# Cross-attention: the second batch's queries of chunks 6 to 9 by seven products for eight, with new softmax sets and a new hand-written order

## The chip, the cores and the metric

The kernel runs on one core of a Trainium2 chip. The metric is device time in microseconds of one execution. Three runs of the kernel before took 495.48, 495.83 and 495.85 us, with a median of 495.83. The engines are called as the profile calls them: PE is TensorE, DVE VectorE, ACT ScalarE, POOL GpSimd, SP the queue that issues DMAs.

## The reference

Two batches of 2048 tokens with 640 channels attend to 154 context rows of 1024 channels. The first 77 context rows are text, the other 77 image rows; each has its own softmax, and the two results are added. There are 20 heads of 32 channels. Everything is fp32.

```python
q    = split_heads(x @ Wq.T)
k, v = split_heads(text @ Wk.T), split_heads(text @ Wv.T)
k_ip, v_ip = split_heads(ip @ Wk_ip.T), split_heads(ip @ Wv_ip.T)
out  = merge(attend(q, k, v)) + merge(attend(q, k_ip, v_ip))
y    = out @ Wo.T + bo + x
```

## The kernel before

**Tiling.** The 640 channels are five chunks of 128, four heads each. Chunk number q counts both batches: 0 to 4 are the first batch's, 5 to 9 the second's. A chunk's 2048 tokens are four blocks of 512; a unit u is half a chunk, 1024 tokens in two blocks (u, h), so chunk q holds units 2q and 2q+1. A unit's scores come in three groups s of 3, 3 and 2 token tiles (of 128), 12 or 8 rows of heads and tiles, each with 2 x 77 scores.

**Stages of a chunk.** `queries` (line 206) makes a block's queries: five matmuls of 512 columns, one for each chunk of input channels, summed in one PSUM bank. `take_queries` (220) scales them into SBUF on ACT. `scores` (242) works on 32-row tiles of the array, four heads at once, into four banks. Then comes the softmax: for most groups ACT copies the scores (254), DVE takes maxima (290), POOL subtracts them (304), ACT takes exponentials (310), DVE sums (315) and inverts (320), POOL multiplies (325) and DVE transposes (332). Three sets of (unit, group) choose otherwise. In `DIRECT` the maxima are taken and the exponentials read straight from PSUM. In `BIASED` the copy stays, but the maximum is the bias of small exponentials (278, one row of 77 each). Both leave out POOL's subtraction. In `SUMMED` these small exponentials also accumulate the sums, which takes the sum from DVE. `attend` (341) multiplies a whole chunk with the values, again on 32-row tiles, 160 records in the profile; it is written A.q below.

**Output.** The first batch's output projection already uses seven products for eight (lines 480 to 530), with sums of attention halves on POOL (440) and of weights (410). The second batch's, after attend 9, is a longer scheme of sums (866, 872), 512-column products (887) and additions to the residual (827, 830).

**Buffers.** x has four buffers of 512 tokens, `xs[0]` to `xs[3]`. For the second batch the fourth, `xs[XROOM]`, holds sums of weights, and blocks of x are loaded anew for each chunk into the other three in turn (line 188). Three weight buffers `wqs` take Wq's chunks in turn (194). A value tile `vT` with its transposed copies `vS0` belongs to the first batch. The residual of the second batch is what the last loads left in the three x buffers, and one more load.

**What sets the order.** Nothing is scheduled by a tool: a string `SCHEDULE` names each step, and `emit` writes it to its engine; each engine runs its own steps in that order. `q.u.h@n` makes queries in bank n, `cq` takes them; `R` is scores, `K M S E D I N T` the softmax steps in the order above, `A` and `CA` attend and its copy; `LX`, `LQ`, `VS`, `SF`, `SS` issue DMAs on SP (x, Wq, values, residual in, output); `m`, `cm`, `G`, `W` are the first batch's output products, their additions and sums; `V`, `X`, `F`, `Y` the second's.

Of the kernel before, what the change touches and what calls it, by code (L numbers as in the profile page):

```python
# [20 lines left out]
def kernel(  # L21
# [31 lines left out]
    NH = 2  # L53
    BLK = NH * TB
# [10 lines left out]
        (11, 0), (12, 0), (13, 0), (13, 2), (14, 0), (14, 2), (15, 1), (15, 2), (18, 1), (19, 2),  # L65
    }
    BIASED = {
        (2, 2), (3, 2), (4, 2), (6, 2), (8, 2), (9, 2), (11, 2), (12, 1), (16, 2), (17, 2), (18, 2),
    }
    SUMMED = {  # L70
        (4, 2), (11, 2), (12, 0), (13, 0), (13, 2), (14, 0), (15, 1), (15, 2), (16, 2), (17, 2), (18, 1),
        (18, 2), (19, 2),
# [13 lines left out]
    halves = banks[:G], banks[G:]  # L86
# [16 lines left out]
    vT = const.tile([P, B, LP], F32, name="vT")  # L103
    nc.gpsimd.memset(vT[:, :, 2 * L :], 0.0)
    vS0 = [const.tile([P, LP], F32, name=f"vS0_{n}") for n in range(2)]
# [108 lines left out]

    def take_queries(u, h, pq):
        if (u, h) in EARLY:
            qT = aT[:, EARLY[u, h]]
        else:
            qT = qpool.tile([P, TB], F32, tag="qT", name=f"qT_{u}_{h}")
        nc.scalar.mul(qT, pq, SCALE)  # L220
        qTs[(u, h)] = qT
# [48 lines left out]
    def exponential_of(u, s, ps=None, den=None):  # L270

        n = GROUPS[s][1]
        for g in range(G):
            for t in range(n):
                for x in range(2):
                    row = rows_of(u, s)[:, t * G + g, x]
                    one = t * G + g, slice(x, x + 1)
                    nc.scalar.activation(  # L278
                        row,
                        row if ps is None else rows_in(ps[g], n)[:, t, x],  # L280
                        AF.Exp,
                        bias=maxs[(u, s)][:, *one],
                        accum_out=None if den is None else den[:, *one],
                    )
# [148 lines left out]
    def sum_t(m, b, i):  # L433
# [6 lines left out]
        nc.gpsimd.tensor_tensor(t_of(m, b, i), x, y, ALU.subtract)  # L440
# [144 lines left out]
    for t in range(2):  # L585

        ps = halves[t][G - 2 + t]
# [76 lines left out]
    def emit(word):  # L664
        name, _, where = word.partition("@")
        k, *args = name.split(".")
        x, y = (*(int(a) for a in args if a.isdigit()), None, None)[:2]
        i = int(k[1:]) if k[1:].isdigit() else None
        if k[0] == "R":
            at[name] = halves[int(where)]  # L670
            scores(x, i, at[name])
        elif k == "A":
# [263 lines left out]
```

## Time and profile before

| | |
|---|---|
| median of three runs | 495.83 us |
| span of the profiled execution | 494.6 us |
| HBM read, written | 54.94 MB, 10.49 MB |
| mean granted TensorE clock | 1.000 |

The profile is one execution, so its span and not the median is what its rows add up to; the runs' median lies 1.2 us above it. In rows that group instructions, the columns are line, engine, operation, output<-input, shape and count, then busy time in us, mean ns of one, and the idle time just before them with what ended it. In rows by stage there follow, after the stretch and its length, the busy times of PE, weight loads, DVE, ACT and POOL with their counts, the granted clock, the DMA share and GB/s. An fp32 matmul leaves two records.

### The profile page before, as it was taken

To read this page: it belongs to the slowest core of one execution; us is meant where nothing else is said; L and a number is where in the kernel's file an instruction comes from. 1 tells how busy PE (TensorE), PEld (TensorE's weight loads), DVE (VectorE), ACT (ScalarE), POOL (GpSimd) and SP (SyncE) were. 2 spreads that over 40 slices of the span, in tenths; PEclk is the share of its full clock that TensorE was granted. 3 is DMA by queue.
4 is the path that set the end of the run, shared out by engine and by line. 5 is a ranking of instruction groups with operands and counts; after the bars stand their busy time and mean duration, and the time that the engine had idled before them with its cause. 6 is when DMAs were issued, how large, how long until landed. Compare 5 with 4: busy or idle time off the path is not lost.

```text
span 494.6 us, 10484 instructions
## 1 busy us (share of the span) xinstructions
PE 489.1 (99%) x4116; PEld 287.7 (58%) x4116; DVE 413.9 (84%) x416; ACT 309.5 (63%) x1002; POOL 370.5 (75%) x158
## 2 busy tenths in 40 slices
PE   9999999999999999999999999999999999999997
PEld 5666648558557556456566654754755675444443
DVE  0069989989899989979988896687789898999996
ACT  1275788977687778677899786587889862100000
POOL 0069988988988988879886758475689899798700
PEclk9999999999999999999999999999999999999999
DMA  8992046203241724895540666455550212320125
GB/s 278 350 288 80 17 124 181 67 1 95 62 150 44 247 65 146 270 345 178 161 172 27 215 195 223 134 172 183 184 169 19 90 42 85 129 85 2 42 85 212
DMA packets 67105, 69.38 MB, mean 140 GB/s; under 512 B 5488, under 2 KB 47088, under 8 KB 67056
## 3 DMA queue, kind: packets, MB, share of 16 engines
q1 hardware_dynamic: 66048, 67.54, 43.7%
q10 hardware_dynamic: 1008, 1.18, 0.7%
q8 instruction: 32, 0.52, 0.4%
q14 instruction: 17, 0.14, 0.1%
HBM read 54.94 MB, written 10.49 MB: 132 GB/s over the span
## 4 chain that ended last, share of the span: by engine, by line
PE 96%; DMA 3%; ACTq 0%; ACT 0%; DVE 0%; DVEq 0%; issue 0%
PE bank L206 34%; PE bank L887 12%; PE bank L341 11%; PE bank L242 11%; PE bank L499 10%; PE bank L144 9%; PE bank L480 7%; PE bank L509 3%; DMA aT<-in_L_xattn_Wk_ip_dram 2%; DMA x<-in_x_dram 1%; ACTq L538 0%; ACT pb L254 0%; ACTq L552 0%; DVE acc L830 0%; DVEq L931 0%
## 5 line engine op out<-in xcount | busy, mean ns | idle before, releaser
L325 POOL TENSOR_TENSOR pb<-pb,rden 128x1848 f32<-128x1848 f32 (+1 forms) x60 | 176.0, 2943 | 30.4 <-DVE rden L320 23.6
L304 POOL TENSOR_TENSOR pb<-pb,mx 128x1848 f32<-128x1848 f32 (+1 forms) x39 | 121.6, 3129 | 55.4 <-DVE mx L290 55.3
L206 PE MATMUL bank<-x,wq 128*128 128x512 f32 x280 | 125.4, 598 | 0.1
L332 DVE STREAM_TRANSPOSE pb<-pb 128x1920 f32<-128x1920 f32 (+1 forms) x60 | 115.9, 1938 | 9.1 <-POOL pb L325 8.9
L290 DVE TENSOR_REDUCE mx<-pb 128x24 f32<-128x1848 f32 (+1 forms) x50 | 91.6, 1844 | 32.1 <-ACT pb L254 31.9
L254 ACT COPY pb<-bank 128x462 f32<-128x462 f32 (+1 forms) x200 | 85.3, 542 | 29.3 <-PE bank L242 28.9
L315 DVE TENSOR_REDUCE den<-pb 128x24 f32<-128x1848 f32 (+1 forms) x47 | 88.9, 1895 | 15.6 <-ACT pb L310 12.8
L206 PEld LDWEIGHTS bank<-x,wq 128*128 128x128 f32 x280 | 51.7, 190 | 60.0 <-issue 58.8
L310 ACT ACTIVATE pb<-pb 128x1848 f32<-128x1848 f32 (+1 forms) x39 | 65.6, 1684 | 17.5 <-POOL pb L304 17.4
L278 ACT ACTIVATE pb<-bank,mx 128x77 f32<-128x77 f32 x208 | 60.4, 387 | 6.5 <-DVE mx L293 6.5
L278 ACT ACTIVATE pb<-pb,mx 128x77 f32<-128x77 f32 x184 | 54.1, 356 | 1.9 <-DVE mx L290 1.8
L341 PE MATMUL bank<-pb,v 32*32 32x512 f32 x1600 | 55.2, 597 | 0.0
L206 PE MATMUL bank<-x,aT 128*128 128x512 f32 x116 | 51.8, 596 | 0.0
L242 PEld LDWEIGHTS bank<-kT,qT 32*128 32x128 f32 x1024 | 36.1, 184 | 21.6 <-issue 13.3
L144 PE MATMUL bank<-wo_ct,aT 128*128 128x154 f32 x320 | 46.0, 297 | 0.7 <-DMA aT<-in_L_xattn_Wk_ip_dram 0.4
L144 PEld LDWEIGHTS bank<-wo_ct,aT 128*128 128x128 f32 x320 | 43.0, 188 | 4.7 <-issue 3.0
L242 PE MATMUL bank<-kT,qT 32*128 32x154 f32 x1024 | 45.1, 305 | 0.0
L278 ACT ACTIVATION_READ_ACCUMULATOR pb<-bank,mx 128x1 f32 x168 | 44.0, 266 | 0.0
L341 PEld LDWEIGHTS bank<-pb,v 32*32 32x32 f32 x1600 | 29.0, 103 | 22.7 <-issue 10.1
L480 PE MATMUL bank<-aT,wo_ct 128*128 128x512 f32 x80 | 36.3, 595 | 0.0
L206 PEld LDWEIGHTS bank<-x,aT 128*128 128x128 f32 x116 | 21.4, 190 | 23.7 <-issue 23.5
L220 ACT ACTIVATE qT<-bank 128x512 f32<-128x512 f32 x32 | 19.3, 631 | 23.4 <-PE bank L206 23.4
(83 smaller groups left out, 524.2 us busy)
## 6 DMA issues: line engine op xcount, KB each, us to landing
x<-in_x_dram SPq DMA_DIRECT2D x20, 1280.0 KB, 6.7
out_dram<-acc SPq DMA_DIRECT2D x19, 256.0 KB, 2.9
x<-in_x_dram SPq DMA_DIRECT2D x17, 256.0 KB, 5.9
acc<-in_x_dram SPq DMA_DIRECT2D x16, 256.0 KB, 4.4
out_dram<-x SPq DMA_DIRECT2D x15, 256.0 KB, 2.0
v<-vS SPq DMA_DIRECT2D x160, 20.0 KB, 2.7
aT<-in_L_xattn_Wk_dram SPq DMA_DIRECT2D x5, 512.0 KB, 6.0
aT<-in_L_xattn_Wk_ip_dram SPq DMA_DIRECT2D x5, 512.0 KB, 5.5
```

Source lines behind the costliest of these rows:

```text
L144: nc.tensor.matmul(keys_in(out), loaded[n][:, k, :], cT[:, k, :, t, :], start=(k == 0), stop=(k == NCC - 1))
L206: nc.tensor.matmul(pq, weight_of(q)[:, k, :], xs[place_of(u, h)][:, k, :], start=(k == 0), stop=(k == NC - 1), skip_group_check=loose,)
L242: nc.tensor.matmul(ps[g][:, ts(t, 2 * L)], qTs[(u, h)][g * D : (g + 1) * D, ts(st, P)], kT[g * D : (g + 1) * D, c, b].rearrange("p t l -> ...
L254: nc.scalar.copy(keys_of(u, s)[:, :, g], ps[g][:, : n * 2 * L].rearrange("p (n l) -> p n l", n=n))
L278: nc.scalar.activation(row, row if ps is None else rows_in(ps[g], n)[:, t, x], AF.Exp, bias=maxs[(u, s)][:, *one], accum_out=None if den i ...
L290: nc.vector.tensor_reduce(mx, rows_of(u, s), AX.X, ALU.max, negate=negate)
L304: nc.gpsimd.tensor_tensor(rows_of(u, s), rows_of(u, s), maxs[(u, s)].unsqueeze(3).to_broadcast([P, n, 2, L]), ALU.subtract)
L315: nc.vector.tensor_reduce(den_of(u, s), rows_of(u, s), AX.X, ALU.add)
L325: nc.gpsimd.tensor_tensor(rows_of(u, s), rows_of(u, s), rdens[(u, s)].unsqueeze(3).to_broadcast([P, n, 2, L]), ALU.mult)
L332: nc.vector.transpose(p, p)
L341: nc.tensor.matmul(pa[r][g * D : (g + 1) * D, :], v4s[q % 2][rows, g, k, :], zones[rows, :, g, k, :], start=(k == 0), stop=(k == NK - 1),)
L480: nc.tensor.matmul(ps, wo[:, k, ts(NC - 1, P)], rows_of_attention(b, k)[:, i], start=(k == 0), stop=(k == NC - 1),)
```

## The change

**Queries in pairs.** Chunk 5 keeps its queries as they are. Chunks 6 and 7, and 8 and 9, are made in pairs, block by block of 512 tokens: four of the five chunks of input channels, as a 2 x 2 scheme (output chunk by half of the input, token half by half of the input), take seven products in place of eight; the fifth chunk of input channels is added by four more matmuls. POOL makes the sums of token halves, partly in place in x, and the sums of weights, in place in `wqs`; ACT writes the first part of each quarter of the queries and DVE adds the others. In the order string these steps are `U` (sums of weights), `h` (sums of tokens), `g` (products) and `cg` (their results).

```diff
+    spare = xs[XROOM - 1]
+    t1_spare = v_sb[:, : 2 * HT].rearrange("p (kp t) -> p kp t", kp=2)
+    s4_room = xs[XROOM].rearrange("p k t -> p (k t)")[:, ds(18 * P, 2 * P)]
+    def pair_weights(p):
+        q = NC + 1 + 2 * p
+        a, c, third = (wqs[(q + n) % 3] for n in range(3))
+        return {
+            1: a[:, 0:2],
+            2: a[:, 2:4],
+            3: s4_room.rearrange("p (kp o) -> p kp o", kp=2),
+            4: c[:, 2:4],
+            5: third[:, 0:2],
+            6: third[:, 2:4],
+            7: c[:, 0:2],
+            8: (a[:, NC - 1], c[:, NC - 1], third[:, NC - 1]),
+        }
+    def sum_pair_weights(n, p, eng):
+        w = pair_weights(p)
+        out, x, y, f = (
+            (w[5], w[7], w[4], ALU.add),
+            (w[6], w[5], w[1], ALU.subtract),
+            (w[7], w[1], w[7], ALU.subtract),
+            (w[3], w[2], w[6], ALU.subtract),
+            (w[8][2], w[8][0], w[8][1], ALU.subtract),
+        )[n]
+        eng.tensor_tensor(out, x, y, f)
+    def unit_of(p, i):
+        return SUB * (NC + 1 + 2 * p) + i // NH, i % NH
+    def pair_tokens(p, i):
+        x = xs[place_of(*unit_of(p, i))]
+        b11, b12, b21, b22 = (x[:, 2 * k : 2 * k + 2, SIDES[t]] for k in range(2) for t in range(2))
+        return {1: b11, 2: b21, 3: b22, 4: b21, 5: t1_spare, 6: b11, 7: b12}, (b11, b12, b21, b22), x
+    def sum_pair_tokens(m, p, i, eng):
+        t, (b11, b12, b21, b22), _ = pair_tokens(p, i)
+        x, y = {5: (b12, b11), 6: (b22, t[5]), 7: (b22, b12), 4: (b21, t[6])}[m]
+        eng.tensor_tensor(t[m], x, y, ALU.subtract)
+    def pair_product(m, p, i, ps):
+        w, (t, _, x) = pair_weights(p), pair_tokens(p, i)
+        part = ps[:, :HT]
+        for kp in range(2):
+            nc.tensor.matmul(
+                part,
+                w[m][:, kp],
+                t[m][:, kp],
+                start=(kp == 0 and m in (1, 2, 5)),
+                stop=(kp == 1 and m in (1, 6, 7)),
+                skip_group_check=True,
+            )
+        if m in (2, 3, 4, 5):
+            n, side = {2: (0, 0), 5: (1, 1), 3: (2, 1), 4: (1, 0)}[m]
+            nc.tensor.matmul(
+                part, w[8][n], x[:, NC - 1, SIDES[side]], start=False, stop=True, skip_group_check=True
+            )
+    def take_pair_product(m, p, i, ps):
+        second, side = {1: (0, 0), 2: (0, 0), 6: (0, 1), 3: (0, 1), 5: (1, 1), 7: (1, 1), 4: (1, 0)}[m]
+        u, h = unit_of(p, i)
+        t = query_of(u + SUB * second, h)[:, SIDES[side]]
+        if m in (1, 6, 5, 4):
+            nc.scalar.mul(t, ps[:, :HT], SCALE)
+        else:
+            nc.vector.scalar_tensor_tensor(t, ps[:, :HT], SCALE, t, ALU.mult, ALU.add)
```

**Buffers.** The later chunk's queries wait in x's third buffer; so x is loaded into two buffers in turn from the second batch's fifth block on, each block of a pair once for both chunks, and the residual of three blocks is loaded anew before the last stage (`LH`). The temporary sum of tokens lies where the first batch's values were.

```diff
+    HOMES = (1, 3, 2)
-        return late.index((u, h)) % XROOM if b else sub * NH + h
+        n = late.index((u, h))
+        return (0, 1, 2, 0)[n] if n < NHB else (n + 1) % 2
+            elif b and c and c % 2 == 0:
+                qTs[(u, h)] = spare[:, (sub * NH + h + NHB * (c == NC - 1)) % NC]
-    home = {}
+    home = {i: xs[n] for n, i in enumerate(HOMES)}
+    def load_home(n):
+        tokens = ds(S + HOMES[n] * TB, TB)
+        nc.sync.dma_start(out=xs[n], in_=xT[:, tokens].rearrange("(k p) t -> p k t", p=P))
```

**Sets and order.** `DIRECT` shrinks from 10 to 7 groups, `BIASED` grows from 11 to 16 and `SUMMED` from 13 to 16. Small exponentials are issued by quarters of a group (`E.s.u.g`), scores and attend take any four banks in place of one half of PSUM, and the whole `SCHEDULE` is new.

```diff
-            at[name] = halves[int(where)]
+            at[name] = [banks[int(n)] for n in where]
-        "co.0 T0.10 R2.11@0 K1.11 m5.0@4 I1.10 K2.11 D0.11 N1.10 R1.12@0 M2.11 q.13.0@7 K1.12 I0.11 T1.10 VS.6.1 "
+        "cq.11.0 R2.10@0472 T0.9 K2.10 U0.0 R1.10@1365 h5.0.0 g1.0.0@0 K1.10 T1.9 U1.0 g2.0.0@2 h6.0.0 cg1.0.0 "
```

What this does to the engines is shown at three places. First PE, where the kernel before makes queries of chunks 6 and 7 (wq is the chunk's weights, x_82 to x_85 are x's four buffers):

```order
L206 MATMUL bank_72<-x_83,wq_76 128x512 x5
L206 MATMUL bank_74<-x_84,wq_75 128x512 x5
L499 MATMUL bank_71<-aT,x_85 128x256 x2
L509 MATMUL bank_71<-aT,x_85 128x256
L499 MATMUL bank_71<-aT,x_85 128x256 x2
L509 MATMUL bank_71<-aT,x_85 128x256
```

And PE now, at the first products of the first pair, just before attend 4 (v_sb is the temporary sum of tokens):

```order
L281 MATMUL bank_67<-x_83,wq_75 128x256 x2
L281 MATMUL bank_69<-x_83,wq_75 128x256 x2
L291 MATMUL bank_69<-x_83,wq_75 128x256
L281 MATMUL bank_73<-v_sb,wq_77 128x256 x2
L291 MATMUL bank_73<-x_83,wq_76 128x256
L281 MATMUL bank_67<-x_83,wq_77 128x256 x2
L281 MATMUL bank_69<-x_82,wq_75 128x256 x2
L291 MATMUL bank_69<-x_82,wq_75 128x256
L281 MATMUL bank_72<-x_82,wq_75 128x256 x2
```

The queries' five matmuls of 512 columns have become products of two of 256, some with a third for the fifth chunk, and some read what POOL has summed. POOL before, from the first sum of attention halves on (304 subtracts maxima, 325 multiplies, 410 sums output weights):

```order
L440 TENSOR_TENSOR x_85<-aT 128x512
L304 TENSOR_TENSOR pb<-pb,mx_0_1829 128x12x154
L304 TENSOR_TENSOR pb<-pb,mx_2_1923 128x8x154
L304 TENSOR_TENSOR pb<-pb,mx_1_1926 128x12x154
L325 TENSOR_TENSOR pb<-pb,rden_2_1966 128x8x154
L325 TENSOR_TENSOR pb<-pb,rden_0_1998 128x12x154
L410 TENSOR_TENSOR x_85<-wo_ct 128x512
L410 TENSOR_TENSOR x_85<-x_85,wo_ct 128x512
L410 TENSOR_TENSOR wo_ct<-wo_ct 128x2x2x128
```

POOL now at the same place (262 sums weights, 275 tokens, 405 multiplies):

```order
L405 TENSOR_TENSOR pb<-pb,rden_1_1773 128x12x154
L262 TENSOR_TENSOR wq_77<-wq_76 128x256
L275 TENSOR_TENSOR v_sb<-x_83 128x512
L262 TENSOR_TENSOR wq_77<-wq_77,wq_75 128x256
L275 TENSOR_TENSOR x_83<-x_83,v_sb 128x2x256
L405 TENSOR_TENSOR pb<-pb,rden_2_1789 128x8x154
L275 TENSOR_TENSOR x_83<-x_83 128x2x256
L275 TENSOR_TENSOR v_sb<-x_82 128x512
L275 TENSOR_TENSOR x_83<-x_83 128x2x256
L262 TENSOR_TENSOR wq_76<-wq_75,wq_76 128x256
```

The pair's sums now stand between the softmax steps, and those with x_83 or x_82 as output overwrite what a product has to have read. SP now, around the loads for the second pair (wq_77 and wq_75 are its weights):

```order
L199 DMA wq_77<-in_L_xattn_Wq_dram 128x5x128
L554 DMA out_dram<-res 128x512
L199 DMA wq_75<-in_L_xattn_Wq_dram 128x5x128
L193 DMA x_83<-in_x_dram 128x5x512
L550 DMA acc<-in_x_dram 128x2x256
L193 DMA x_82<-in_x_dram 128x5x512
L548 DMA res<-in_x_dram 128x512
```

The two loads of x alternate between x_83 and x_82, where x_84 was the third before, and follow two loads of weights.

More of the change, by code (lines that the diff above doesn't have):

```diff
@@ L64 @@
     DIRECT = {
-        (11, 0), (12, 0), (13, 0), (13, 2), (14, 0), (14, 2), (15, 1), (15, 2), (18, 1), (19, 2),
+        (1, 2), (9, 1), (11, 0), (13, 0), (15, 1), (18, 1), (19, 2),
     }
     BIASED = {
-        (2, 2), (3, 2), (4, 2), (6, 2), (8, 2), (9, 2), (11, 2), (12, 1), (16, 2), (17, 2), (18, 2),
+        (4, 0), (6, 0), (7, 2), (10, 1), (11, 1), (12, 0), (12, 1), (12, 2), (13, 2), (14, 1), (15, 2), (16, 2),
+        (17, 2), (18, 0), (18, 2), (19, 1),
     }
     SUMMED = {
-        (4, 2), (11, 2), (12, 0), (13, 0), (13, 2), (14, 0), (15, 1), (15, 2), (16, 2), (17, 2), (18, 1),
-        (18, 2), (19, 2),
+        (1, 2), (4, 0), (6, 0), (7, 2), (9, 1), (10, 1), (11, 1), (12, 1), (12, 2), (14, 1), (15, 1), (15, 2),
+        (17, 2), (18, 1), (19, 1), (19, 2),
     }
@@ L85 @@
     banks = [psum.tile([P, TB], F32, name=f"bank_{n}") for n in range(2 * G)]
-    halves = banks[:G], banks[G:]
     wqs = [const.tile([P, NC, P], F32, name=f"wq_{n}") for n in range(3)]
@@ L101 @@
     nc.gpsimd.memset(pb[:, :, :, :, 2 * L :].rearrange("p z n g l -> p (z n g) l"), 0.0)
-    vT = const.tile([P, B, LP], F32, name="vT")
+    v_sb = const.tile([P, 4 * LP], F32, name="v_sb")
+    vT = v_sb[:, : B * LP].rearrange("p (b l) -> p b l", b=B)
     nc.gpsimd.memset(vT[:, :, 2 * L :], 0.0)
-    vS0 = [const.tile([P, LP], F32, name=f"vS0_{n}") for n in range(2)]
+    vS0 = [v_sb[:, ds((B + n) * LP, LP)] for n in range(2)]
     vS1 = const.tile([P, NC, LP], F32, name="vS1")
@@ L182, in place_of @@
         _, b, _, sub = step_of(u)
-        return late.index((u, h)) % XROOM if b else sub * NH + h
+        if not b:
+            return sub * NH + h
+        n = late.index((u, h))
+        return (0, 1, 2, 0)[n] if n < NHB else (n + 1) % 2
     def load_block(u, h):
@@ L213, in queries, with query_of @@
             )
-    def take_queries(u, h, pq):
-        if (u, h) in EARLY:
-            qT = aT[:, EARLY[u, h]]
-        else:
-            qT = qpool.tile([P, TB], F32, tag="qT", name=f"qT_{u}_{h}")
-        nc.scalar.mul(qT, pq, SCALE)
-        qTs[(u, h)] = qT
+    def query_of(u, h):
+        if (u, h) not in qTs:
+            _, b, c, sub = step_of(u)
+            if (u, h) in EARLY:
+                qTs[(u, h)] = aT[:, EARLY[u, h]]
+            elif b and c and c % 2 == 0:
+                qTs[(u, h)] = spare[:, (sub * NH + h + NHB * (c == NC - 1)) % NC]
+            else:
+                qTs[(u, h)] = qpool.tile([P, TB], F32, tag="qT", name=f"qT_{u}_{h}")
+        return qTs[(u, h)]
@@ new lines, in take_queries @@
+    def take_queries(u, h, pq):
+        nc.scalar.mul(query_of(u, h), pq, SCALE)
+    spare = xs[XROOM - 1]
[14 more added lines that the diff above has]
+        }
@@ L268, in den_of, with exponential_of @@
         return dens[(u, s)]
-    def exponential_of(u, s, ps=None, den=None):
+    def exponential_of(u, s, g, ps=None, den=None):
         n = GROUPS[s][1]
[L273 to L284, printed above, removed]
+        for t in range(n):
+            for x in range(2):
+                row = rows_of(u, s)[:, t * G + g, x]
+                one = t * G + g, slice(x, x + 1)
+                nc.scalar.activation(
+                    row,
+                    row if ps is None else rows_in(ps[g], n)[:, t, x],
+                    AF.Exp,
+                    bias=maxs[(u, s)][:, *one],
+                    accum_out=None if den is None else den[:, *one],
+                )
     def maxima(u, s, ps=None, negate=False):
@@ L431, in t_of, with sum_t @@
         return sums[:, (5, 7, 6, 4).index(m)].rearrange("p (kp t) -> p kp t", kp=2)
-    def sum_t(m, b, i):
+    def sum_t(m, b, i, eng):
         x, y = {
@@ L585 @@
     for t in range(2):
-        ps = halves[t][G - 2 + t]
+        ps = banks[G * t + G - 2 + t]
         project_kv(t, ps)
@@ L668, in emit @@
         i = int(k[1:]) if k[1:].isdigit() else None
+        adder = nc.vector if args and args[-1] == "d" else nc.gpsimd
         if k[0] == "R":
-            at[name] = halves[int(where)]
+            at[name] = [banks[int(n)] for n in where]
             scores(x, i, at[name])
         elif k == "A":
-            at[name] = halves[int(where)]
+            at[name] = [banks[int(n)] for n in where]
             attend(x, at[name])
@@ L682, in emit @@
             load_block(x, y)
+        elif k == "LH":
+            load_home(x)
         elif k == "LQ":
@@ L701, in emit @@
                 elif direct or biased:
-                    exponential_of(
-                        x, i, ps if direct else None, den_of(x, i) if (x, i) in SUMMED else None
-                    )
-                else:
+                    if (x, i) in SUMMED and (x, i) not in dens:
+                        den_of(x, i)
+                    exponential_of(x, i, int(args[1]), ps if direct else None, dens.get((x, i)))
+                elif args[1] == "0":
                     exponential(x, i)
@@ L725, in emit @@
             store_last(at[name[1:]], 0, x)
+        elif k[0] == "U":
+            sum_pair_weights(i, x, adder)
+        elif k[0] == "h":
+            sum_pair_tokens(i, x, y, adder)
+        elif k[0] == "g":
+            at[name] = banks[int(where)] if where else at[f"g{JOINS[i]}.{x}.{y}"]
+            pair_product(i, x, y, at[name])
+        elif k[:2] == "cg":
+            take_pair_product(int(k[2:]), x, y, at[name[1:]])
         elif k[0] == "m":
@@ L733, in emit @@
         elif k[0] == "G":
-            sum_t(i, 0, x)
+            sum_t(i, 0, x, adder)
         else:
@@ L847, in finish @@
         elif k == "LA":
-            for u, h in late[-XROOM:]:
-                home[step_of(u)[3] * NH + h] = xs[place_of(u, h)]
             (fourth,) = set(range(NHB)) - set(home)
```

2 lines of the change are left out of this document (1 added, 1 removed), and 149 rows, old and new, of the table SCHEDULE.

## The prediction, made before the change was run

> **What bounds the kernel now.** I read the page first: its span, its busy times, the chain that ended last.
>
> ```profile
> span 494.6 us, 10484 instructions
> PE 489.1 (99%) x4116; PEld 287.7 (58%) x4116; DVE 413.9 (84%) x416; ACT 309.5 (63%) x1002; POOL 370.5 (75%) x158
> PE 96%; DMA 3%; ACTq 0%; ACT 0%; DVE 0%; DVEq 0%; issue 0%
> ```
>
> TensorE is busy for 489.1 of 494.6 us and holds 96% of the chain; the 5.5 us left lie at both ends. So the time is what TensorE has to do, as long as nobody makes it wait. A busy matmul can hide a wait, since a record's duration is longer than its share of the pipe, so I read the chain next, in a stretch of the second batch (start, length, what).
>
> ```profile
> 239.84 0.43 PE bank L499 x2
> 240.28 1.00 PE bank L242 x24
> 241.27 8.78 PE bank L206 x20
> 250.05 0.86 PE bank L499 x4
> 250.92 0.43 PE bank L509 x2
> 251.35 0.86 PE bank L499 x4
> 252.21 0.43 PE bank L509 x2
> 252.64 0.74 PE bank L242 x16
> 253.38 1.92 PE bank L499 x8
> 255.30 5.45 PE bank L341 x150
> 260.76 1.06 PE bank L499 x4
> ...
> 324.73 8.58 PE bank L206 x20
> ```
>
> Each fp32 matmul leaves two records. Twenty 512-column records take 8.58 us, 0.429 each, so a matmul of 512 columns costs **0.858 us**. Four 256-column records take 0.86, so one of 256 columns costs **0.43 us**: half. There are no gaps; what is lost is lost where the array changes to 32-row tiles and back. Sixteen score records stand for 0.74 us and twenty-four for 1.00, 0.0325 each; the block after them is 0.20 longer than without (8.78 against 8.58, 1.92 against 8 x 0.215). An excursion to the tiles and back thus costs 0.74 + 0.20 - 16 x 0.0325 = **0.42 us** beside its records.
>
> Last I read the busy time of each engine by stage, cut where an attend starts (columns: PE, weight load, DVE, ACT, POOL).
>
> ```profile
> 27.00:69.00 42.00, 42.00 (x297) 25.88 (x311) 39.31 (x29) 28.65 (x61) 38.19 (x13) 1.00 0.43 117
> 143.00:178.00 35.00, 35.00 (x392) 20.98 (x386) 33.53 (x26) 26.21 (x57) 30.33 (x11) 1.00 0.40 120
> 387.00:422.00 35.00, 35.00 (x338) 23.44 (x352) 29.98 (x37) 19.47 (x78) 33.37 (x19) 1.00 0.25 81
> 210.50:421.90 211.40, 211.37 (x1896) 127.98 (x1906) 178.04 (x191) 161.59 (x658) 166.72 (x73) 1.00 0.47 151
> ```
>
> In the first batch VectorE is busy for 33.53 of 35 us (95.8%), before the last attend GpSimd for 33.37 of 35 (95.3%), and TensorE waits in neither. From attend 4 to attend 9, where the change lands, GpSimd is at 166.7 of 211.4 us, 79%.
>
> **The change, part by part.** *TensorE.* Chunks 6 to 9 of the second batch are two pairs with four blocks of 512 tokens each. A block of a pair took 2 x 5 matmuls of 512 columns; now seven products of two matmuls and four fifth-row matmuls, all of 256 columns, 18 in all.
>
> ```profile
> L206 PE MATMUL bank<-x,wq 128*128 128x512 f32 x280 | 125.4, 598 | 0.1
> L206 PE MATMUL bank<-x,aT 128*128 128x512 f32 x116 | 51.8, 596 | 0.0
> ```
>
> The 396 records are 198 matmuls; 80 of them go: 80 x 0.858 = 68.6 us. 144 of 256 columns come: 144 x 0.43 = 62.0. The difference is **-6.6 us**. The durations in the rows are no price: a record of 256 columns lasts 379 ns and one of 512 lasts 592, but they overlap; the chain's spacing counts.
>
> The Trainium skill (TensorE: Matmul & The Clock Gate, Back-to-back issue gap) gives 262 cycles for 256 columns against 518 for 512, a bit over half. By that ratio the 144 would cost 62.5 us and the gain would be 6.1; the trace's 0.43 against 0.858 is nearer to an exact half, and the measurement decides.
>
> The new order also has more changes of shape: counted in the instruction orders, stretches of tiled work between full-array work go from 50 to 52, and places where attend and score tiles follow each other directly from 6 to 5. An excursion more is 0.42, a joint less saves about half of one: 2 x 0.42 - 0.2 = **+0.6 us**.
>
> *GpSimd.* It gets 32 sums of token halves and ten of weights.
>
> ```profile
> L440 POOL TENSOR_TENSOR aT<-aT x8: 1264/1272/1282, 250.3 to 397.9; 128x512 f32<-128x512 f32 x8
> L410 POOL TENSOR_TENSOR x<-wo_ct 128x256 f32<-128x256 f32 x1 | 0.7, 731 | 0.0
> L866 POOL TENSOR_TENSOR pb<-wo_ct 128x128 f32<-128x128 f32 x4 | 1.9, 492 | 0.2 <-PE bank L341 0.2
> L304 POOL TENSOR_TENSOR pb<-pb,mx 128x1848 f32<-128x1848 f32 x13 | 42.7, 3288 | 20.4 <-DVE mx L290 20.4
> L304 POOL TENSOR_TENSOR pb<-pb,mx 128x1232 f32<-128x1232 f32 x2 | 4.5, 2253 | 0.2 <-DVE mx L290 0.2
> ```
>
> Between attends 4 and 9 stand 28 token sums (28 x 1.272 = 35.6 us) and eight weight sums (6 x 0.731 + 2 x 0.492 = 5.4). The last two rows are of that stage alone: 13 long and 2 short subtractions; by the new sets 9 and 3 are left there, -13.2 + 2.3. GpSimd has 166.7 + 35.6 + 5.4 - 10.9 = 196.8 us to do while TensorE has 211.4 - 6.0 = 205.4: **95.8%**. That is the share at which the two stages above ran, each over 35 us, without TensorE waiting, so I cost it at nothing, but there is little cover left; its price is a rival below.
>
> *ScalarE and VectorE.* Of a block's seven results ScalarE takes four and VectorE adds three.
>
> ```profile
> L220 ACT ACTIVATE qT<-bank 128x512 f32<-128x512 f32 x32 | 19.3, 631 | 23.4 <-PE bank L206 23.4
> L368 ACT COPY aT<-bank 128x256 f32<-128x256 f32 x40 | 11.4, 403 | 16.5 <-PE bank L341 16.5
> L278 ACT ACTIVATE pb<-pb,mx 128x77 f32<-128x77 f32 x184 | 54.1, 356 | 1.9 <-DVE mx L290 1.8
> L278 ACT ACTIVATION_READ_ACCUMULATOR pb<-pb,mx 128x1 f32 x80 | 16.1, 202 | 0.0
> L524 DVE SCALAR_TENSOR_TENSOR acc<-bank,bo_sb,acc 128x256 f32<-128x256 f32 x32 | 13.5, 465 | 2.4 <-PE bank L509 2.3
> ```
>
> ScalarE: 32 x 0.403 - 16 x 0.631 = +2.8 us. VectorE: 24 x 0.465 = +11.2, of which a part comes back, since 44 softmax sums are left to it in place of 47. By the new sets ScalarE also has 88 more exponentials of one row each, all with an accumulator to read: 88 x (54.1 / 184 + 0.2) = 43 us over the whole program, with 37 whole-group exponentials left of 39. Both keep more room than GpSimd in this stage (178.0 and 161.6 of 211.4 before), so they cost nothing by themselves; without that cover an addition on VectorE would cost its 0.465 us.
>
> *DMA.* Loads of x for the second batch go from 20 to 12, and three come for the residual, so there is less to move. But two buffers now alternate, and a block can be loaded only once the last product that reads the old one is done. I added up TensorE's instructions between that product and the first of the new block: 10.1 and 10.6 us for the last two blocks of the first pair, 10.4, 20, 37 and 8.5 for the second pair's.
>
> ```profile
> DMA to landing us min/median/max: 6.1/6.7/13.6
> ```
>
> At 6.7 us every block is in time; at 13.6, seen where three such loads followed each other, four would be late. I take the median, with 0 to 5 us as ends.
>
> *The rest.* Free choice of banks, scores in another order, softmax split by quarters: off TensorE's path, between no gain and the waits that they cause. For those I take the stage with the fullest DMA queues.
>
> ```profile
> 200.00:250.00 50.00, 49.88 (x437) 27.56 (x436) 44.76 (x42) 37.94 (x130) 44.03 (x19) 1.00 0.73 242
> ```
>
> 0.12 us idle in 50, over 205 us: **+0.5**. The start and the closing stage hold the same work; the last matmuls, the last two additions and the store stay as they are.
>
> ```profile
> 490.07 1.03 PE L887 MATMUL bank<-pb,wo_ct 128*128 128x256 f32 x4
> 491.13 0.75 DVE L830 TENSOR_TENSOR acc<-acc,bank 128x256 f32<-128x256 f32 x2 [0.31 <-PE bank L887]
> 491.91 0.35 ACTq L836 DMA_DIRECT2D out_dram<-acc  x1
> ```
>
> The sum: -6.6 + 0.6 + 0.5 = **-5.5 us**. The profiled span of 494.6 becomes 489.1. The runs' median is 495.8, 1.2 above it for what lies outside the span, so the time is **490.3 us**.
>
> **The rivals.** *A block of x comes late.* For: the windows of 8.5 to 10.6 us, one of them right behind two weight loads in the same queue. Against: fewer bytes, and a median of 6.7. One load at 13.6 costs 13.6 - 8.5 = 5.1 at most, 3 to 4 elsewhere: 491.5 to 495.4.
>
> *GpSimd becomes the bound, and the kernel is slower.* It works in order; a sum that overwrites a half of x must wait until a product has read it, and the normalisations queued behind it feed the transposes and then the attend. If it can be kept busy only for 90.9% (38.19 of 42 us, as in the first stage above), 196.8 us of work take 216.5, 11.1 more than TensorE needs: 501.4. It decides from 95.8% down, and from 93.1% (196.8 / 211.4) the gain is gone. Against it: the 95.3% before the last attend, on the same engine, shows that 90.9% is no ceiling; that stage was 35 us long, though, not 205.
>
> The Trainium skill (SBUF — State Buffer, Who interferes with whom) says that a VectorE instruction with two inputs in SBUF and a GpSimd instruction that reads SBUF block each other. Here VectorE's new additions read one operand from PSUM, so by that rule the token sums keep their duration; the narrow spread of 1264 to 1282 ns agrees, and this speaks against this rival.
>
> *It does not do what it says:* the 256-column matmuls cost more than half. At the ratio of the durations, 379 to 592, they would cost 144 x 0.55 = 79 us and the time 507. The chain's rows speak plainly against it.
>
> *More than forecast:* the new order also removes the excursions' extra cost and the short waits: 488.5.
>
> **How the numbers follow.** Forecast, 489.0 to 491.5: 0.64. Late block: 0.14 (0.12 faster, 0.02 within). GpSimd bound: 0.15, of which 0.05 eat a part of the gain, 0.02 end within, 0.08 slower. Half price wrong: 0.02. More: 0.05. About 0.2% is what a measurement of this kernel can tell from no change, 494.8 to 496.8. Faster: 0.64 + 0.12 + 0.05 + 0.05 = 0.86; within: 0.04; slower: 0.10. The range of 488.6 to 496.0 leaves out the slow part of the GpSimd case, the wrong price and some of the last case, 0.13.
>
> **What would show it.** TensorE's chain without gaps, 256-column records at 0.215 us, and query lines with 6.6 us less in sum, would show the gain. GpSimd near 96% in the stage of attends 4 to 9, with TensorE's idle time there under 1 us, would show that it holds; waits of weight loads on GpSimd's pair sums or on loads of x, or a chain that passes through POOL or DMA, would show a rival. A closing stage that has become longer would make the forecast wrong in a place that I took as unchanged.

## The result, and the profile after

| | before | after |
|---|---|---|
| median of 4 runs each, us | 495.84 (495.48 to 496.14) | 491.46 (491.06 to 491.92) |
| span of the profiled execution, us | 494.6 | 490.1 |

The changed kernel takes 0.991 of the time of the one before (interval 0.9896 to 0.9924): 4.4 us faster, where 5.5 were forecast. The page of the kernel after, its span, the share of busy time and the chain that ended last:

```profile
span 490.1 us, 11003 instructions
PE 483.0 (99%) x4244; PEld 311.9 (64%) x4244; DVE 408.8 (83%) x428; ACT 339.9 (69%) x1204; POOL 402.3 (82%) x198
PE 69%; POOL 10%; DVE 9%; DMA 5%; ACT 4%; issue 2%; ACTq 0%; SPq 0%; DVEq 0%; POOLq 0%
```

TensorE is still busy for all but 7.1 us, but its share of the chain has fallen from 96% to 69%. That is not lost time: the chain leaves TensorE wherever the last thing to be ready was another engine's, be it by 0.2 us, and then follows that engine's work, which lies beside TensorE's. What is lost must be read from the waits. First the price of a matmul, from the chain of the kernel after (start, length, what; L211 are queries of 512 columns, L281 products of 256):

```profile
50.67 4.29 PE bank L211 x10
...
250.45 0.86 PE bank L281 x4
251.74 0.86 PE bank L281 x4
...
262.77 1.73 PE bank L281 x8
```

0.429 us a record for 512 columns, 1.73 / 8 = 0.216 for 256, as forecast. By the cycles that the Trainium skill gives (TensorE: Matmul & The Clock Gate, Back-to-back issue gap), which the prediction weighed, an estimate of the second is 0.429 x 262 / 518 = 0.217, so this spacing can't tell that ratio from an exact half, 0.215.

Next four stretches of the kernel after (length, then busy time of PE, weight load, DVE, ACT, POOL, the granted clock, DMA share and GB/s). Attends 2, 3, 4 and 9 start at 144.4, 177.8, 213.5 and 416.6 us here, so the third stretch begins 4.2 us ahead of attend 4, with the first pair's products:

```profile
143.00:178.00 35.00, 34.38 (x380) 19.42 (x394) 31.92 (x25) 29.25 (x79) 30.51 (x11) 1.00 0.63 197
178.00:209.30 31.30, 31.04 (x363) 19.48 (x336) 26.94 (x25) 26.83 (x87) 29.37 (x14) 1.00 0.40 120
209.30:417.10 207.80, 207.58 (x2033) 152.35 (x2036) 183.99 (x200) 185.72 (x767) 198.11 (x111) 1.00 0.38 119
417.00:487.00 70.00, 69.12 (x310) 30.75 (x278) 61.51 (x99) 2.31 (x8) 40.05 (x24) 1.00 0.26 94
```

In the long stretch GpSimd is busy for 198.1 of 207.8 us, 95.3%, and TensorE idle for 0.22. Exactly from attend 4 to attend 9 GpSimd is busy for 193.5 of 203.1 us, again 95.3%, where 196.8 of 205.4, 95.8%, were forecast. TensorE's idle time stands elsewhere: 0.62 and 0.26 us in the two stretches before it, 0.88 in the closing one, of which 0.54 lie behind the last matmul. The attends themselves say where the time went: attend 4 starts 3.0 us later than before (part of the first pair's products now stands ahead of it), attend 9 starts 211.4 us after attend 4 before and 203.1 now (-8.3), and from attend 9 to the last matmul it is 68.9 before and 69.5 now (+0.6).

The view of TensorE's waits in the kernel after (who waited for whom: us in total, times, longest; two waits on DMAs at the start, and one that the kernel before has as well, are left out):

```profile
PE bank L323 <- ACT kT L826: 0.6, 1, 0.6
...
PE bank L1006 <- DVE res L944: 0.3, 1, 0.3
PE bank L146 <- ACT aT L448: 0.3, 1, 0.3
PE bank L421 <- DVE pb L412: 0.2, 1, 0.2
```

Such a row counts idle time, and records overlap, so a wait costs a bit more than its row. I added up, from the starts of successive records, what each gap has above the usual spacing: 0.69 us at 165.1 (for chunk 4's keys), 0.33 at 184.0 (for a bank that ScalarE still copies from), 0.29 at 212.9 (for the transpose ahead of attend 4), 0.14 at 252.2 and 0.51 at 429.4 (for the residual): 1.96 us. In the kernel before the same sum has 0.16. The waits of the first 20 us are counted in neither.

Two of them by the timeline of the kernel after (start, length, engine, line, operation; in brackets the idle time before it and who ended it). At 165 us, ScalarE's copy of the keys and what waits for it:

```profile
165.64 0.34 ACT L358 ACTIVATE pb<-pb,mx 128x77 f32<-128x77 f32 x1
165.89 0.18 ACT L358 ACTIVATION_READ_ACCUMULATOR pb<-pb,mx 128x1 f32 x1
165.98 0.26 ACT L826 COPY kT<-bank 128x154 f32<-128x154 f32 x1
166.29 1.46 PE L323 MATMUL bank<-kT,qT 32*128 32x154 f32 x36 [0.62 <-ACT kT L826]
```

The copy takes 0.26 us and comes behind the small exponentials of a group that the new sets have put there. The second is at 429 us; the chain of the kernel after shows how it comes about:

```profile
409.19 5.51 POOL pb L405 x2
...
416.16 1.18 DVE x L991
417.34 0.80 DVE acc L604 x2
...
418.58 4.49 DMA out_dram<-acc
...
423.61 5.74 DMA res<-in_x_dram
...
429.44 0.76 DVE res L944
430.33 1.95 PE bank L1006 x4
```

The load of the residual stands in SP's queue behind a load into `acc`, which must wait until the last store from `acc` has landed; that store waits for VectorE's sums, and these for GpSimd's normalisations. So a late GpSimd shows up some 15 us behind its own work, which ended at 414.70. The load itself is no new one. It stands in the kernel before (first line) as in the kernel after (second line), from the timelines of the queue that issues DMAs:

```profile
423.41 0.50 SPq L855 DMA_DIRECT2D res<-in_x_dram  x1
423.61 0.49 SPq L974 DMA_DIRECT2D res<-in_x_dram  x1
```

It is issued at the same time in both, but attend 9 starts at 421.8 us before and at 416.6 after. TensorE gets there 5 us earlier, and the load does not.

The loads of x, in the kernel after:

```profile
DMA to landing us min/median/max: 6.1/6.6/8.6
```

The 10.1, 10.6, 10.4, 20, 37 and 8.5 us that the prediction counted between a block's last product and the first of the next were enough; no wait of TensorE is put down to a load of x.

### The profile page after: what moved, and what is told of

It is laid out like the page before. It is cut to its first block, busy times and chain, and to the rows that moved or that the text cites. A ratio compares the mean times of both kernels' runs of the same rounds, so it can differ in the third digit from the quotient of the medians.

```text
span 490.1 us, 11003 instructions
## 1 busy us (share of the span) xinstructions
PE 483.0 (99%) x4244; PEld 311.9 (64%) x4244; DVE 408.8 (83%) x428; ACT 339.9 (69%) x1204; POOL 402.3 (82%) x198
## 4 chain that ended last, share of the span: by engine, by line
PE 69%; POOL 10%; DVE 9%; DMA 5%; ACT 4%; issue 2%; ACTq 0%; SPq 0%; DVEq 0%; POOLq 0%
PE bank L1006 11%; PE bank L211 11%; PE bank L281 10%; PE bank L579 9%; PE bank L323 8%; PE bank L421 7%; PE bank L146 5%; POOL pb L405 5%; POOL pb L384 4%; PE bank L560 4%; DVE pb L412 3%; PE bank L291 3%; PE bank L589 2%; DVE den L395 2%; DMA aT<-in_L_xattn_Wk_ip_dram 2%
## 5 line engine op out<-in xcount | busy, mean ns | idle before, releaser
L384 POOL TENSOR_TENSOR pb<-pb,mx 128x1848 f32<-128x1848 f32 (+1 forms) x37 | 110.0, 2980 | 33.8 <-DVE mx L370 33.8
L358 ACT ACTIVATE pb<-pb,mx 128x77 f32<-128x77 f32 x328 | 104.7, 373 | 1.9 <-DVE mx L370 1.7
L335 ACT COPY pb<-bank 128x462 f32<-128x462 f32 (+1 forms) x212 | 90.5, 544 | 14.5 <-PE bank L323 14.4
L395 DVE TENSOR_REDUCE den<-pb 128x24 f32<-128x1848 f32 (+1 forms) x44 | 81.4, 1854 | 11.9 <-ACT pb L390 9.2
L390 ACT ACTIVATE pb<-pb 128x1848 f32<-128x1848 f32 (+1 forms) x37 | 59.3, 1618 | 18.9 <-POOL pb L384 18.8
L211 PE MATMUL bank<-x,wq 128*128 128x512 f32 x120 | 54.1, 599 | 0.0
L211 PE MATMUL bank<-x,aT 128*128 128x512 f32 x116 | 51.8, 596 | 0.0
L358 ACT ACTIVATION_READ_ACCUMULATOR pb<-pb,mx 128x1 f32 x232 | 49.2, 212 | 0.0
L358 ACT ACTIVATE pb<-bank,mx 128x77 f32<-128x77 f32 x152 | 42.9, 382 | 1.2 <-DVE mx L373 1.1
L281 PE MATMUL bank<-x,wq 128*128 128x256 f32 x160 | 41.4, 387 | 0.0
L211 PEld LDWEIGHTS bank<-x,wq 128*128 128x128 f32 x120 | 21.9, 189 | 24.7 <-issue 24.7
L211 PEld LDWEIGHTS bank<-x,aT 128*128 128x128 f32 x116 | 21.5, 190 | 24.1 <-issue 23.8
L323 PEld LDWEIGHTS bank<-kT,qT 32*128 32x128 f32 x768 | 26.9, 184 | 13.8 <-issue 8.2
L281 PEld LDWEIGHTS bank<-x,wq 128*128 128x128 f32 x160 | 29.3, 190 | 7.3 <-issue 3.6
```

The costliest lines, as they stand in the source:

```text
L211: nc.tensor.matmul(pq, weight_of(q)[:, k, :], xs[place_of(u, h)][:, k, :], start=(k == 0), stop=(k == NC - 1), skip_group_check=loose,)
L281: nc.tensor.matmul(part, w[m][:, kp], t[m][:, kp], start=(kp == 0 and m in (1, 2, 5)), stop=(kp == 1 and m in (1, 6, 7)), skip_group_check ...
L323: nc.tensor.matmul(ps[g][:, ts(t, 2 * L)], qTs[(u, h)][g * D : (g + 1) * D, ts(st, P)], kT[g * D : (g + 1) * D, c, b].rearrange("p t l -> ...
L335: nc.scalar.copy(keys_of(u, s)[:, :, g], ps[g][:, : n * 2 * L].rearrange("p (n l) -> p n l", n=n))
L358: nc.scalar.activation(row, row if ps is None else rows_in(ps[g], n)[:, t, x], AF.Exp, bias=maxs[(u, s)][:, *one], accum_out=None if den i ...
L384: nc.gpsimd.tensor_tensor(rows_of(u, s), rows_of(u, s), maxs[(u, s)].unsqueeze(3).to_broadcast([P, n, 2, L]), ALU.subtract)
```

## Experiments

The theory after the result: the 6.6 us of matmuls are gone as forecast, and about 2 us come back as waits, of which the new sets and order cause some and the full GpSimd the others. Rivals: the products cost more than forecast and fewer waits were added; or GpSimd sets the pace of the whole stage. Beside the first four experiments the kernel before, on the same chip, took 496.76 us (495.73 to 496.94), beside the last four, on another chip, 495.94 (495.63 to 497.18).

**Eight products in the new order.** Everything stands where it stands in the changed kernel, but a block's products use the weights and token halves themselves, eight products for seven, and GpSimd's sums do nothing.

```diff
+        a11, a12, a21, a22 = w[1], w[2], w[7], w[4]
+        parts, n, side = {
+            1: (((a11, b11),), None, 0),
+            2: (((a12, b21),), 0, 0),
+            6: (((a11, b12),), None, 1),
+            3: (((a12, b22),), 0, 1),
+            5: (((a21, b12),), 1, 1),
+            7: (((a22, b22),), None, 1),
+            4: (((a21, b11), (a22, b21)), 1, 0),
+        }[m]
...
         elif k[0] == "U":
-            sum_pair_weights(i, x, adder)
+            pass
         elif k[0] == "h":
-            sum_pair_tokens(i, x, y, adder)
+            pass
```

> The changed kernel's order, sets, banks and results, but the pairs' queries by eight products of raw weights and raw tokens (20 matmuls of 256 columns for a block in place of 18), and none of GpSimd's 42 sums. Theory (TensorE is the bound, and the gain is the products'): 8 blocks x 2 x 0.431 = 6.9 us more than the changed kernel's 491.5, so 498.4, that is 2.5 us slower than before, since the new order alone costs 2 excursions and the waits that the profile shows. Rival (the new order brings the gain, and the sums cost what the products save): 492 or less.

Measured: 500.31 us, ratio 1.007 (1.0055 to 1.0085), 3.5 us slower than the kernel before where 2.5 were expected; span 498.1, 8.0 above the changed kernel's. The 16 matmuls more account for 16 x 0.43 = 6.9; its waits, read as above, sum to 3.0 against 1.96, so 1.0 more. Together 7.9 of the 8.0. So the saving is real and is all the change has. Against the kernel before, this kernel shows what order, sets and buffers alone cost: 498.1 - 494.6 = +3.5 us, of which 2.8 are waits (3.0 less the 0.16 of before). GpSimd has no sums to make here (356.2 us of work for 402.3), so the sums have no part in these waits. They are not all the changed kernel's, though: 0.82 us stand ahead of attend 9, where it has none, and 0.95 at 437 us, its 0.51 at 429. Both come through GpSimd's last normalisations, as in the chain above, and yet GpSimd is busy for only 153.7 of the 211.1 us between attends 4 and 9, 73%. So a share of 95% is not needed for such waits; why they are longer here stays open.

**No sums.** Seven products, but GpSimd's sums are left out, so the queries of chunks 6 to 9 are not the reference's.

```diff
         elif k[0] == "U":
-            sum_pair_weights(i, x, adder)
+            pass
         elif k[0] == "h":
-            sum_pair_tokens(i, x, y, adder)
+            pass
```

> The changed kernel without GpSimd's sums for the pairs: the seven products read what lies in their places, so the queries of chunks 6 to 9 are not the reference's. Theory (the sums are covered; of the 1.96 us that TensorE waits only about 0.4 lie between attends 4 and 9): 491.1 to 491.5. Rival (GpSimd at 95% is what holds the kernel): 490.0 or less, and the waits at 165, 184, 213 and 429 us are gone.

Measured: 490.65 us (490.00 to 492.01), ratio 0.9878 (0.9857 to 0.9900), between what theory and rival expected; span 489.5, 0.6 below the changed kernel's. The same stretch as the third above, in the kernel without sums:

```profile
209.30:417.10 207.80, 207.73 (x2032) 152.63 (x2038) 183.76 (x200) 185.87 (x768) 153.72 (x71) 1.00 0.38 119
```

And TensorE's waits in this kernel (the second row is a load at the start; the one that the kernel before has as well is left out):

```profile
PE bank L323 <- ACT kT L826: 0.6, 1, 0.6
PE bank L657 <- DMA aT<-in_L_xattn_Wq_dram: 0.5, 1, 0.5
PE bank L146 <- ACT aT L448: 0.3, 1, 0.3
```

GpSimd is down to 153.7 us of work, 74%, and from attend 4 to attend 9 this kernel takes 203.1 us as with the sums. What goes are the waits at 213 and at 429 us, 0.29 + 0.51 = 0.8. The two rows for ScalarE's copies stay: they stand ahead of the first sum. From attend 0 to the last matmul this kernel takes 417.0 us, the changed one 418.0. So 46 us of work on GpSimd cost 0.8 to 1.0 us by the traces. By the ratios to the kernel before it would be 1.6, but their intervals overlap, so the runs' times bear out no more than that it is little.

**One sum made twice.** The fifth product's token sum is made a second time in all eight blocks, 8 x 1.27 = 10.2 us more for GpSimd.

```diff
             sum_pair_tokens(i, x, y, adder)
+            if i == 5:
+                sum_pair_tokens(i, x, y, adder)
```

> The changed kernel with one token sum of each block (the one into the temporary buffer) made twice on GpSimd: 8 x 1.27 = 10.2 us more for GpSimd between attends 4 and 9, 198 + 10 = 208 us of work in about 204. Theory (GpSimd is just below the bound, with no more than some 5 us of room): TensorE waits, 2 to 5 us slower than the changed kernel, 493.5 to 496.5. Rival (there is room for as much again, since GpSimd's idle time is spread over waits that nobody minds): 491.5 to 492.

Measured: 498.86 us, ratio 1.0044 (1.0029 to 1.0059); span 497.1, +7.0, more than the 2 to 5 that the theory allowed. The stage from attend 4 to attend 9, and TensorE's waits, in this kernel:

```profile
215.00:423.90 208.90, 205.04 (x1986) 149.29 (x1986) 179.39 (x196) 183.18 (x753) 202.29 (x114) 1.00 0.35 110
```

```profile
PE bank L281 <- POOL x L275: 2.0, 3, 1.2
PE bank L421 <- DVE pb L412: 1.5, 2, 1.0
...
PE bank L323 <- ACT pb L358: 0.6, 1, 0.6
PE bank L281 <- DVE qT L302: 0.6, 1, 0.6
```

10.2 us of added work cost 7.0. GpSimd's share between these attends has risen only from 95.3 to 202.29 / 208.90 = 96.8%: the stage grows with its work. Now TensorE waits for the sums themselves and for the transposes behind GpSimd's normalisations.

**Products of half the width.** The 112 product matmuls of 256 columns are made as two of 128.

```diff
         for kp in range(2):
+            for c in range(2):
                 nc.tensor.matmul(
-                    part,
+                    part[:, ts(c, HT // 2)],
                     w[m][:, kp],
-                    t[m][:, kp],
+                    t[m][:, kp, ts(c, HT // 2)],
```

> The changed kernel with each of the products' 112 matmuls of 256 columns issued as two of 128 columns with the same weights. Theory (price by columns, as for 512 against 256, and as the 154-column rows at 0.132 us a record suggest): 0 to 3 us slower than the changed kernel, 491.5 to 494.5. Rival (the weight load of 0.19 us becomes the floor of a record): 448 records x (0.19 - 0.108) = 37 us slower, about 528.

Measured: 492.04 us, ratio 0.9905 (0.9891 to 0.9920); span 490.5, +0.4. In the chain of this kernel (L282 are its products):

```profile
220.53 0.89 PE bank L282 x8
...
263.11 1.78 PE bank L282 x16
```

A record of 128 columns takes 0.111 us where one of 256 takes 0.216. The price goes nearly by columns down to here (a quarter of 0.429 would be 0.107), so the rival of a wrong half price falls, with room to spare. The +0.4 is not the whole price of the narrower products: from attend 4 to attend 9 this kernel takes 204.1 us for 203.1, and the waits at 213 and 429 us are gone although every sum is made, because TensorE gets to these places later.

**The changed kernel again**, beside the next three on another chip.

> The changed kernel itself, to stand beside the three below on one chip: 0.991 of before, with the same waits of TensorE at about 165, 184, 213 and 429 us.

Measured: 491.06 us (490.78 to 491.75), ratio 0.9902 (0.9888 to 0.9915); span 489.5. The waits are the same ones: 0.69, 0.34, 0.28, 0.14 and 0.34 us. (The view of waits puts the last down to a sum of GpSimd's, but in both profiles TensorE goes on some 0.14 us behind the end of the residual's addition.) The span is 0.6 shorter than in the first profile; 0.4 of that is gone before attend 0, where the two profiles wait for different loads. Its stage from attend 4 to attend 9, to set beside the two kernels with added sums:

```profile
213.00:416.10 203.10, 203.06 (x1986) 148.74 (x1986) 179.50 (x196) 183.72 (x758) 193.53 (x107) 1.00 0.37 114
```

**Two waits taken away.** The copy of chunk 4's keys stands four small exponentials earlier (not twelve, as expected below: of the steps that it passes only `E2.7.1` is one of small exponentials), and the residual's load stands ahead of the load into `acc` instead of behind it.

```diff
-... E1.7.0 E0.7.3 E1.7.1 E1.7.2 D0.7 I0.7 N0.7 E2.7.1 ck.4.0 cq.9.0 ...
+... E1.7.0 E0.7.3 ck.4.0 E1.7.1 E1.7.2 D0.7 I0.7 N0.7 E2.7.1 cq.9.0 ...
...
+            nc.sync.dma_start(out=res, in_=xT[ts(NC - 1, P), ds(S + fourth * TB, TB)])
             nc.sync.dma_start(
...
             )
-            nc.sync.dma_start(out=res, in_=xT[ts(NC - 1, P), ds(S + fourth * TB, TB)])
```

> The changed kernel with two steps moved: ScalarE copies chunk 4's second keys 12 small exponentials earlier, and the residual's last 128 channels are loaded before the other 512. Theory (the two longest waits, 0.69 us at 165 and 0.51 us at 429, are these two steps coming late): both are gone and the kernel is 1.0 to 1.2 us faster than the changed kernel on the same chip. Rival (GpSimd's chain sets the pace, so that a wait taken away comes back at the next attend): no gain, 0 to 0.3 us, with a longer wait before attend 4 or 5.

Measured: 490.66 us (490.50 to 491.18), ratio 0.9891 (0.9876 to 0.9906). The median is 0.4 below that of the changed kernel beside it, with overlapping intervals, so it can't be told from it; 1.0 to 1.2 were expected. From attend 0 to the last matmul it takes 417.3 us, the changed kernel 418.0 and 417.8 in its two profiles. In the trace the closing stage's wait is gone, and attend 9 to the last matmul takes 68.9 us, as in the kernel before. ScalarE at the other place, in this kernel:

```profile
162.92 1.75 ACT L390 ACTIVATE pb<-pb 128x1848 f32<-128x1848 f32 x1 [1.10 <-POOL pb L384]
164.57 0.27 ACT L826 COPY kT<-bank 128x154 f32<-128x154 f32 x1
164.74 0.36 ACT L358 ACTIVATE pb<-pb,mx 128x77 f32<-128x77 f32 x1
```

The copy comes 1.4 us earlier, and of the wait of 0.69 there remain 0.28, at 166.3: the next thing on TensorE is late in its turn. The timeline of its weight loads says which:

```profile
166.75 0.82 PEld L323 LDWEIGHTS bank<-kT,qT 32*128 32x128 f32 x18 [0.36 <-ACT qT L232]
```

The next scores wait for a block of queries, which ScalarE takes from 166.12 to 166.70 us, now behind the same four small exponentials. So moving the load worked fully, moving the copy partly.

**The fifth sums on VectorE.** One of a block's four token sums goes from GpSimd to VectorE.

```diff
-            sum_pair_tokens(i, x, y, adder)
+            sum_pair_tokens(i, x, y, nc.vector if i == 5 else adder)
```

> The changed kernel with eight of the 32 token sums, the ones into the temporary buffer, on VectorE in place of GpSimd: 8 x 1.27 = 10.2 us less for GpSimd, about 8 x 0.65 = 5 us more for VectorE. Theory (GpSimd has about 3 us of room and holds TensorE for no more than some tenths): no change within 0.5 us of the changed kernel. Rival one (GpSimd sets the pace): 0.6 to 1.2 us faster, like the run without sums. Rival two (VectorE has no room at these places, or the two engines shut each other out, so that the sums last longer than 0.7 us beside GpSimd's work): 1 us or more slower.

Measured: 493.88 us, ratio 0.9959 (0.9946 to 0.9972): 2.8 us slower than the changed kernel beside it, though GpSimd has 8 us less to do. The moved sums (duration in ns: min, median, max), and TensorE's longest wait in this kernel:

```profile
L275 DVE TENSOR_TENSOR v_sb<-x x8: 648/792/1860, 206.6 to 345.3; 128x512 f32<-128x512 f32 x8
```

```profile
PE bank L579 <- DVE acc L604: 1.9, 1, 1.9
```

The timeline of the slowest of the eight, with GpSimd's two instructions beside it:

```profile
245.28 2.26 POOL L384 TENSOR_TENSOR pb<-pb,mx 128x1232 f32<-128x1232 f32 x1
247.49 2.71 POOL L405 TENSOR_TENSOR pb<-pb,rden 128x1232 f32<-128x1232 f32 x1
```

```profile
246.23 1.86 DVE L275 TENSOR_TENSOR v_sb<-x 128x512 f32<-128x512 f32 x1
248.01 0.86 DVE L604 SCALAR_TENSOR_TENSOR acc<-bank,bo_sb,acc 128x256 f32<-128x256 f32 x2
249.58 2.07 DVE L370 TENSOR_REDUCE mx<-pb 128x24 f32<-128x1848 f32 x1
```

The sum starts at 246.23; GpSimd's subtraction ends at 247.54, and the sum 0.55 later; alone, as at 306.0 us, it takes 0.65 in all. GpSimd's next instruction in turn takes 2.71 us where this form takes 2.26 on average in the changed kernel. The Trainium skill (SBUF — State Buffer, Who interferes with whom) says that a VectorE instruction with two inputs in SBUF contends with a GpSimd instruction that reads SBUF, and that this contention is an exclusive lock; this trace agrees in both directions. Four of the eight sums have a GpSimd instruction beside them for long, and take 0.90 to 1.86 us. The delay pushes VectorE's queue back: the wait of 1.9 us at 251.9 is one of TensorE for an addition into `acc` that stands two maxima behind the sum. How much of the 2.8 us comes from this holding up, and how much from the 5.2 us of work that VectorE gets even without it, was not separated.

**One sum twice in half of the blocks**, 5.1 us more for GpSimd.

```diff
             sum_pair_tokens(i, x, y, adder)
+            if i == 5 and y in (1, 3):
+                sum_pair_tokens(i, x, y, adder)
```

> The changed kernel with four token sums made twice in place of eight, 5.1 us more for GpSimd. Eight cost about 7 of 10.2 us, so that 3.2 us found room. Theory (one common room in the whole stage): 5.1 - 3.2 = 2 us slower than the changed kernel. Rival (each sum is waited for at its place, a fixed share of its duration): 5.1 x 0.69 = 3.5 us slower.

Measured: 494.51 us, ratio 0.9966 (0.9954 to 0.9979); 3.45 above the changed kernel beside it, two thirds of what was added, as with 10.2 us. By the traces, from attend 0 to the last matmul, it is 2.9 of 5.1. Its stage from attend 4 to attend 9:

```profile
213.40:419.50 206.10, 204.34 (x1986) 149.29 (x1986) 179.20 (x196) 183.74 (x758) 198.48 (x111) 1.00 0.36 112
```

96.3% on GpSimd. A common reserve of 3.2 us would have left a cost of 2.0, so my theory isn't borne out: each added microsecond costs some 0.6 to 0.7. A reserve of about 1 us can't be ruled out. Nor does the cost come where the work is added: the second sums start at 214.3, 246.4, 306.6 and 346.5 us, and the two longest new waits of TensorE, 1.1 and 0.8 us, end at attend 5 (269.8) and among the scores at 336.8. Both experiments double the same sum; added work at another place of GpSimd's order was not tried.

## Why the prediction was right, and where it was off

- **The matmuls, -6.6.** Right. The spacings are those of the forecast (by the mean ones, 0.4291 and 0.2158, it is -6.5), and undoing the seven products alone gives 8.0 us back with its own waits, of which 6.9 are the 16 matmuls by their price.
- **Changes of shape, +0.6.** Not measured by itself. What the sums above leave over is -4.5 + 6.6 - 1.8 = +0.3, and +0.3 in the kernel of eight products as well (3.5 - 2.8, less 0.4 since its 320 records of 0.2158 us replace 160 of 0.4291).
- **Short waits, +0.5.** This is the term that was off: 1.96 - 0.16 = 1.8 us. I had taken it from one stage of before, for the long stage of after, and there it was about right (0.29 + 0.14). Two of the waits, 0.69 and 0.33, stand before attend 4: I had seen that the new sets give ScalarE more work, and compared that with its room over the whole stage, though for the first of the two a single short copy of keys behind the small exponentials is enough to stop TensorE. (The 43 us were too many as well. An exponential and its accumulator's read overlap the next, at 0.34 us a pair in the lines above where I had added up 0.49, and ScalarE's busy time rose by 30.4 us.) The third, 0.51, stands in the closing stage, which I had set down as holding the same work. The load that is waited for was there before; what is new is that TensorE reaches it 5 us earlier while the load still waits for GpSimd's normalisations. Issuing it ahead of the load into `acc` removed the wait.
- **GpSimd at nothing, "but there is little cover left".** The first half held nearly (0.8 to 1.0 us by the traces, through the transpose before attend 4 and the residual), and so did the second: taking away 46 us gains about 1, adding 5.1 costs 3.45. That the kernel came out so near the edge is luck in part. The cover was taken from two stretches of 35 us, of which only one is GpSimd's, and the kernel of eight products waits through GpSimd at 73%, so the share alone doesn't tell where the edge is. The rival in which GpSimd becomes the bound and the kernel slower than before was wrong for this amount of work, and right with a quarter more token sums (40 for 32: ratio 1.0044).
- **Late block of x.** Did not happen; the landing times were at most 8.6 us.
- **Half price wrong.** Did not happen, and doesn't even at a quarter.
- **The token sums' duration.** It was expected to stay in spite of VectorE's additions, and did: 1266 to 1297 ns after, against 1264 to 1282 for the like sums of before.
- **More than forecast.** Did not happen. Its 488.5 us do not follow from the sum either: without the 0.6 and the 0.5 it gives 489.2.

The forecast of -5.5 against -4.4 is thus near for the right reason in its largest term, and off by the waits. What stays open: whether the wait at 184 us, for a copy by ScalarE that stands behind GpSimd's subtractions in the chain, and the 0.28 us left at 166.3 us can be had away; neither was tried. That the span differs by 0.6 us between two executions of the same kernel also limits how far the last 0.3 us can be split.

## What to carry to other kernels

Read the cover that an engine gives from both sides: here GpSimd took 46 us of sums, up to 95% of a stage, for about 1 us, and doubling one of these sums then cost some two thirds of the added time. A share of busy time over a long stage doesn't show a 0.26 us copy that stands in the wrong place of a queue; for each engine whose work grows, look at what TensorE needs next from that queue. A stage isn't unchanged when the busiest engine reaches it earlier: follow each of its loads back to what the load waits for, and ask whether that comes earlier too.

## What the runs showed of the hardware that was not expected

The weight loads of the kernel with products of half the width (count, busy us, mean ns):

```profile
L282 PEld LDWEIGHTS bank<-x,wq 128*128 128x128 f32 x320 | 40.0, 191 | 5.0 <-issue 3.6 <-ACT pb L336 0.2 <-ACT x L301 0.2
```

Matmuls of 128 columns in fp32 cost 0.111 us a record, about half of 256 columns' 0.216, although each weight load lasts 0.191 us: the duration of a load sets no floor there. And VectorE and GpSimd held each other up by large parts of an instruction, 1.31 us of a 1.86 us sum; it met four of the eight sums, and with sums that are twice as fast by themselves (0.65 against 1.27 us) the kernel was slower.
